# A planner's transfer lengths: by size instead of one length for each transfer

## The chip, the cores and the metric

The kernel runs on one core of a Trainium2 chip. Its engines are TensorE (PE in the profile; PEld is its weight load), VectorE (DVE), ScalarE (ACT), GpSimd (POOL) and SyncE (SP), which here issues the transfers of the main loop. The metric is the device time of one execution in microseconds (us), the median of several runs; lower is better. Times inside an execution come from one profiled run.

## What is computed

Two layers follow each other on an input of 8 images, 192 channels, 64 x 64 pixels, all in float32. The first is a gated scan over four directions, the second an attention over windows of 8 x 8 pixels with an MLP. Cut to what matters:

```python
# layer 0
x = conv1x1(x, W_in)                                  # 192 -> 384 channels
x = depthwise_conv3x3(x, W_dw) + b_dw
proxy = conv1x1(x, W_xd)                              # 384 -> 16
Gl, Gm, Gr = normalize_w(*split(conv1x1(proxy, W_w))) # each / (|Gl|+|Gm|+|Gr|+1e-7)
Ls, Us, Ds = (conv1x1(proxy, w) for w in (W_l, W_u, W_d))
xs = [x, x.T, flip(x), flip(x.T)]                     # four directions
# columns are cut into chunks of 8; the scan runs over the 8 places in a chunk
h = l * x + gl * h_up + gm * h + gr * h_dn
y = sum_d w_m[d] * (out * Us + xs * Ds)
x = conv1x1(grn(layernorm2d(y)), W_out)               # grn: norm over the whole image
# layer 1
s = layernorm(x); q, k, v = s @ qkv_w.T, in windows of 64 tokens, 6 heads
attn = softmax(top16(l2n(q) @ l2n(k).T * temp) + rpb)
x2 = s + (attn @ v) @ proj_w.T
out = x2 + gelu(layernorm(x2) @ fc1_w.T) @ fc2_w.T
```

## The kernel before

Each image passes through three stages, and three images are in work at once.

`front(b)` makes the first two lines. In four reads it loads rows of x into `xt` (L505, L506). For each of three channel tiles ct it projects them on PE, ScalarE copies the result into `xin`, and SP stores that in an HBM buffer `pad` with a border (L539). For the convolution SP loads strips of `pad`, three shifted copies of 132 KB each, into one of two `strip` buffers (L553), and PE multiplies them at L565, 24 matmuls for a strip. ScalarE writes two layouts of the result, `st` and `sn`, and SP stores them in the HBM buffers `xs` and `xsT` (L598, L599). An image has 24 stores of `pad`, 48 strips, and 24 stores each of `xs` and `xsT`. `pad` is there twice, `xs` and `xsT` three times.

`scan(b)` has 8 steps t, each over 12 tiles (direction d, channel tile ct). At the start of a step `proxy` loads all of x0 from `xs` (L631), multiplies it on PE (L638), and carries the small result through HBM (`flat`, L653) to a spread copy `xe` (L661). The nine tiles of directions other than 0 each load an `xd` of 256 KB (L694), in one of four buffers. PE makes the gates at L678; ScalarE, VectorE and GpSimd take their absolute values, normalise them and update the state `hid` between L711 and L807; `dx` and `hu` (L833, L838) are the outputs, and GpSimd sums them into `y3`. `norm` finishes a step, and SP stores it in the HBM buffer `z` (L928). The scan of an image can start only when its whole `xs` is written.

`window_row(b, g)` handles one of the 8 rows of windows: it loads `zg` from `z` into a single buffer (L1032), ScalarE scales it (L1037), PE turns it into tokens (L1052), and then attention and MLP follow up to the stores of `out` (L1513, L1516). It needs the norm over the whole image, so it starts after that image's scan.

None of this is written in the order in which it runs. Every piece is handed to a planner, `Plan`, as a step: engine, cost, function, what it reads and what it writes. `written_down` gives the steps a first rank, so that scan b, windows b - 1 and front b + 1 lie beside each other. `Plan.order` then plays the whole program through 12 times: `run` keeps, for every engine, the time at which it is free, takes the step that can start within 40 ns of that time and has the lowest rank (or else the one that can start first), and notes its start. After each run the rank of a step becomes the latest start that its users allow, and the shortest of the 12 runs wins. The steps are sorted by their planned start, and each engine gets its instructions in that order; from then on the order is fixed, and on the chip only semaphores hold it back.

The cost of a step on any engine but PE is a pair: how long it holds its engine, and how much later its result is there.

```python
hold, more = s.cost
free[e] = t + hold
s.end = free[e] + more
```

SP is such an engine, and a transfer is such a step. Before, `dma(n)` gives n transfers a hold of 350 ns each and 2600 ns more, whatever their size. A user on another engine is ready 70 ns (`HOP`) after that.

Of the kernel before, what the change touches and what calls it, by code (L numbers as in the profile page):

```python
# [288 lines left out]
def tile_ss2d_then_window_attention(ctx: ExitStack, tc: tile.TileContext, a: dict, out: bass.AP):  # L289
# [6 lines left out]
    nc = tc.nc  # L296
# [61 lines left out]
    xt = blank("xt", [P, 3, 8, W])  # L358
# [16 lines left out]
    with tc.tile_pool(name="prep", bufs=2) as prep, tc.tile_pool(name="prep_ps", bufs=2, space=PSUM) as prep_ps:  # L375
# [12 lines left out]
        for n, pair in enumerate(PAIRS):  # L388
            for k, (d, _) in enumerate(pair):
                w = w_g2[64 * k : 64 * k + 64, n * P : (n + 1) * P]  # L390
# [51 lines left out]
        for ci in range(2):  # L442
            w = w_f1[:, ci, :]
# [15 lines left out]
    plan = Plan()  # L459
# [3 lines left out]
    mm = lambda slots, n, share=1.0: (slots * n * 4.0, share)  # L463

    mg = lambda share=1.0: (512 * 5.0 + 240, share)
    dma = lambda n=1: (350.0 * n, 2600.0)
    tiny = (150.0, 90.0)
    log_c = {}
    log_half = blank("log_half", [P, 1], math.log(0.5) / 3)
# [25 lines left out]
    def front(b, xs, xsT):  # L495
        xb = x[b]
        padded = pad[b % 2]

        def read(s):


            def get():
                for k in range(2):
                    rows = slice(8 * (s + k), 8 * (s + k) + 8)
                    nc.sync.dma_start(xt[:, k], xb[0:P, rows, :])  # L505
                    nc.sync.dma_start(xt[64 * k : 64 * k + 64, 2], xb[P:DM, rows, :])  # L506

            plan("SP", dma(4), get, w=["xt", (xs, "room"), (xsT, "room")])

        def project(ct, s):  # L510

            own = padded[ct * P : (ct + 1) * P]
            cols = slice(ct * P, (ct + 1) * P)
            pins = [bank() for _ in range(2)]

            def products():
                outs = [p().rearrange("p (h w) -> p h w", h=8) for p in pins]
                for k in range(2):
                    nc.tensor.matmul(outs[k], lhsT=w_in[:, 0, cols], rhs=xt[:, k], start=True, stop=False)
                for k in range(2):  # L520
                    half = slice(64 * k, 64 * k + 64)
                    nc.tensor.matmul(outs[k], lhsT=w_in[half, 1, cols], rhs=xt[half, 2], start=False, stop=True)

            plan("PE", mm(3, 512), products, r=["xt"], w=pins)
            for k in range(2):
                cur, pin = xin[k], pins[k]
                plan(
                    "ACT",
                    act(512),
                    lambda cur=cur, pin=pin: nc.scalar.copy(  # L530
                        cur[:, :, 1 : W + 1], pin().rearrange("p (h w) -> p h w", h=8)
                    ),
                    r=[pin],
                    w=[("xin", k)],
                )
                plan(
                    "SP",
                    dma(),
                    lambda cur=cur, row=8 * (s + k) + 1: nc.sync.dma_start(own[:, row : row + 8, :], cur),  # L539
                    r=[("xin", k)],  # L540
                    w=[("pad", b % 2, ct, s + k)],
                )

        def convolve(ct, s):

            own = padded[ct * P : (ct + 1) * P]
            pc = bank()
            for k in range(2):
                strip = strips[k]

                def read(row=8 * s + 4 * k, strip=strip):
                    for dy in range(3):
                        nc.sync.dma_start(  # L553
                            strip[dy * RG : (dy + 1) * RG],
                            own[:, row + dy : row + dy + 4, :].rearrange("(q m) h w -> m q (h w)", m=RG),
                        )

                near = [("pad", b % 2, ct, n) for n in range(max(0, s + k - 1), min(NG, s + k + 1))]
                plan("SP", dma(3), read, r=near, w=[("strip", k)])
                rows4 = strip.rearrange("p q (h w) -> p q h w", h=4)  # L560

                def products(k=k, rows4=rows4):
                    for dx in range(3):
                        for q in range(4):
                            nc.tensor.matmul(  # L565
                                pc()[q * RG : (q + 1) * RG, k * 256 : (k + 1) * 256].rearrange("p (h w) -> p h w", h=4),
                                lhsT=w_cv[:, ct, q, dx, :],
                                rhs=rows4[:, q, :, dx : dx + W],
                                start=dx == 0,
                                stop=dx == 2,  # L570
                            )

                plan("PE", mm(3, 256), products, r=[("strip", k)], w=[(pc, k)])
            rows = slice(s * 64, (s + 1) * 64)
            st = Held(fpool, [P, CH, 64], "st")
            plan(
                "ACT",
                (1060.0, 120.0),
                lambda: nc.scalar.activation(
                    st().rearrange("p t (i c) -> p i c t", c=CH),  # L580
                    pc().rearrange("p (i c t) -> p i c t", c=CH, t=CH),
                    AF.Identity,
                    bias=b_dw[:, ct : ct + 1],
                ),
                r=[pc],
                w=[st],
            )
            sn = Held(fpool, [P, 8, W], "sn")
            plan(
                "ACT",  # L590
                act(512),
                lambda: nc.scalar.activation(
                    sn(), pc().rearrange("p (h w) -> p h w", h=8), AF.Identity, bias=b_dw[:, ct : ct + 1]
                ),
                r=[pc],
                w=[sn],
            )
            plan("SP", dma(), lambda: nc.sync.dma_start(xs()[:, ct, :, rows], st()), r=[st], w=[(xs, ct, s)])  # L598
            plan("SP", dma(), lambda: nc.sync.dma_start(xsT()[:, ct, :, rows], sn()), r=[sn], w=[(xsT, ct, s)])  # L599

        for s in range(0, NG + 1, 2):
            if s < NG:
                read(s)
            for ct in range(CT):
                if s < NG:
                    project(ct, s)
                    yield
                for k in range(max(0, s - 1), min(NG, s + 1)):
                    convolve(ct, k)
                    yield  # L610


    def scan(b, xs, xsT, z, made):
# [14 lines left out]
        def proxy(t):  # L628

            x0 = Held(spool, [P, CT, 512], "x0", bufs=1)  # L630
            plan("SP", dma(), lambda: nc.sync.dma_start(x0(), xs()[:, :, t, :]), r=[xs], w=[x0])  # L631
            px = bank()

            def products():
# [19 lines left out]
                r=[xq],  # L654
                w=[flat],
# [6 lines left out]
                r=[flat],  # L662
                w=[xe],
# [7 lines left out]
                r=[xe],  # L671
                w=[xo],
# [9 lines left out]
        def tile_of(t, d, ct, xp, x0, y3, last):  # L682

            ch = d * DIN + ct * P
            if d == 0:
                xd = x0
                flat = lambda: x0()[:, ct, :]
            else:
                xd = Held(spool, [P, 512], "xd", bufs=4)
                src = xs if d == 2 else xsT  # L690
                plan(
                    "SP",
                    dma(),
                    lambda: nc.sync.dma_start(xd(), src()[:, ct, CH - 1 - t if d >= 2 else t, :]),  # L694
                    r=[(src, ct, s) for s in range(NG)],
                    w=[xd],
                )
                flat = lambda: xd()
# [15 lines left out]
            else:  # L714
                g = [bank("g") for _ in range(2)]
# [15 lines left out]
                for r in range(2):  # L731
# [4 lines left out]
                        r=[g[r]],  # L736
                        w=[(ab, r)],
                    )

                def by_state(dst, src, row, n):  # L740
# [13 lines left out]
                    r=[nb, h_key],  # L754
                    w=[(pr, 2)],
                )
                plan("ACT", act(512), lambda: nc.scalar.activation(nb(), nb(), AF.Abs), w=[nb])  # L757
                for r in range(2):
# [4 lines left out]
                        r=[g[r], h_key],  # L763
                        w=[(pr, r)],
# [96 lines left out]
        def norm(t, y3):  # L861
# [14 lines left out]
            def spread(dst, src):  # L876
# [15 lines left out]
                r=[pm],  # L892
                w=[y3],
# [8 lines left out]
            v, r, rr = lambda: pv()[:, 0:P], lambda: sq()[:, 0, 0:P], lambda: sq()[:, 1, 0:P]  # L902
# [7 lines left out]
                r=[sq],  # L910
                w=[pv],
# [5 lines left out]
                r=[pv],  # L917
                w=[sq],
# [6 lines left out]
                r=[pv],  # L925
                w=[y3],
            )
            plan("SP", dma(), lambda: nc.sync.dma_start(z()[:, :, t, :], y3()), r=[y3], w=[(z, t)])  # L928
            for ct in range(CT):
                plan(  # L930
                    "ACT",
# [9 lines left out]
                    r=[y3],  # L941
                    w=[(sq, ct), (gx, ct, t)],
# [11 lines left out]
        for t in range(CH):  # L954
            x0, xe, xo = ready
            y3 = Held(spool, [P, CT, 512], "y3", bufs=2)
# [52 lines left out]
    def window_row(b, g, z, sc, bb):  # L1009
# [19 lines left out]


        zg = Held(lpool, [P, CT, CH, 64], "zg", bufs=1)
        plan("SP", dma(), lambda: nc.sync.dma_start(zg(), z()[:, :, :, g * 64 : (g + 1) * 64]), r=[z], w=[zg])  # L1032

        def scaled_up():
            for ct in range(CT):
# [5 lines left out]
        for t2 in range(2):  # L1041
            pz = bank()
            ss = Held(small, [P, 2], "ss")
            for k in range(2):
# [19 lines left out]
                r=[pz],  # L1064
                w=[(s0, t2)],
            )

            def squares(pz=pz, ss=ss):
# [9 lines left out]
                w=[ss],  # L1078
# [17 lines left out]
        for tt in range(NT):  # L1096
            pq = bank()

            def projected(tt=tt, pq=pq):
# [11 lines left out]
                r=[pq],  # L1111
                w=[(qk, tt)],
# [366 lines left out]
        for ci in range(2):  # L1479
# [35 lines left out]
                    for k in range(2):  # L1515
                        nc.sync.dma_start(o[P:DM, :, 32 * k : 32 * k + 32], ot()[64 * k : 64 * k + 64])  # L1516

            plan("SP", dma(1 + ci), put, r=[ot], w=[("out", b, g, ci)])
            yield
        plan.lane = 1  # L1520

# [110 lines left out]
```

## Time and profile before

| | |
|---|---|
| median of 3 runs | 8295.51 us (8274.17 to 8303.1) |
| the profiled execution, by the clock of the runs | 8293.82 us |
| its span, first to last instruction | 8292.0 us |
| mean granted TensorE clock | 0.827 |
| moved by the 16 DMA engines | 695.70 MB, 84 GB/s in the mean |

The span is what the views of the trace are read against; 1.8 us lie around it. In the views a group has the line, the engine, the tiles as output<-input, and counts or times in us. A wait is written as "engine line <- what ended it: total, times, longest". "PEclk" or "clock" is the share of full speed that TensorE was granted.

The main transfers of the loop, all issued by SP, with their number and size each:

| transfer | line | number | KB each |
|---|---|---|---|
| strip<-pad | L553 | 1152 | 132 |
| xd<-xsT, xd<-xs | L694 | 384 + 192 | 256 |
| pad<-xin | L539 | 192 | 264 |
| xs<-st, xsT<-sn | L598, L599 | 192 + 192 | 256 |
| x0<-xs (x<-xs in the profile) | L631 | 64 | 768 |
| z<-y, zg<-z | L928, L1032 | 64 + 64 | 768 |
| xt<-x | L505, L506 | 64 + 64 | 256, 128 |
| out<-ot | L1513, L1516 | 64 + 128 | 256, 64 |
| flat<-xq, xe<-flat | L653, L661 | 64 + 64 | 64, 256 |

### The profile page before, as it was taken

What the parts mean: (1) busy time and instruction counts of PE and PEld (TensorE: products, weight loads), DVE (VectorE), ACT (ScalarE), POOL (GpSimd) and SP (SyncE); (2) the same over time, 40 slices, a digit from 0 to 9 for tenths busy, and PEclk for the clock granted to TensorE, in tenths of its full rate; (3) what the DMA queues carried; (4) which work ended last, traced back from release to release, by engine and by line L of the source; (5) the groups of instructions that cost most, each with busy time, mean ns of one, the idle gap of its engine ahead of it and who ended that gap; (6) DMA issues with size and microseconds to landing.
All of it is one profiled execution on the core that took longest, in us unless ns stands there. A gap on an engine that the chain in (4) does not pass through costs nothing.

```text
span 8292.0 us, 147108 instructions
## 1 busy us (share of the span) xinstructions
PE 6951.0 (84%) x51224; PEld 3600.7 (43%) x51224; DVE 6381.9 (77%) x15421; ACT 5488.0 (66%) x12537; POOL 5859.7 (71%) x5918
## 2 busy tenths in 40 slices
PE   5677688788988898888988898888888789888887
PEld 2333344444444444444444444444444444444454
DVE  1366777888788987888788887888888888888643
ACT  1355346766677666777577766777677676677787
POOL 0377877788778877788778777778788788877411
PEclk8887579788898788888898889888788887778898
DMA  6776146111542135411532126311111112111110
GB/s 175 193 191 180 42 128 165 50 44 45 139 129 74 52 96 138 107 45 56 157 103 77 46 76 171 91 46 46 57 41 50 43 41 66 41 48 41 30 22 15
DMA packets 1037948, 695.70 MB, mean 84 GB/s; under 512 B 704115, under 2 KB 860214, under 8 KB 1037206
## 3 DMA queue, kind: packets, MB, share of 16 engines
q1 hardware_dynamic: 1035830, 684.99, 30.9%
q8 instruction: 407, 6.67, 0.3%
q14 instruction: 335, 2.74, 0.1%
q10 hardware_dynamic: 1376, 1.30, 0.1%
HBM read 453.43 MB, written 232.67 MB: 83 GB/s over the span
## 4 chain that ended last, share of the span: by engine, by line
PE 23%; ACT 15%; DVE 14%; POOL 9%; DMA 5%; issue 4%; SPq 0%; POOLq 0%; DVEq 0%; ACTq 0%
PE g L678 6%; PE lp L1487 3%; PE lp L1453 2%; ACT at L1286 2%; ACT at L1298 2%; DMA zg<-z 2%; POOL pr L796 2%; PE lp L1052 2%; PE lp L565 2%; DVE pr L742 1%; PE lp L1102 1%; POOL pr L781 1%; ACT ab L735 1%; DMA strip<-pad 1%; POOL ab L766 1%
## 5 line engine op out<-in xcount | busy, mean ns | idle before, releaser
L678 PE MATMUL g<-xe,w_g 32*128 32x512 f32 x3648 | 1281.3, 777 | 284.0 <-DVE dx L833 90.3
L678 PE MATMUL g<-xo,w_g 32*128 32x512 f32 x3648 | 1218.2, 767 | 270.1 <-DVE dx L833 154.0
L796 POOL TENSOR_TENSOR pr<-pr,rr 128x512 f32<-128x512 f32 x672 | 872.5, 1298 | 369.4 <-ACT rr L779 320.5
L781 POOL TENSOR_TENSOR pr<-pr 128x512 f32<-128x512 f32 x672 | 887.2, 1321 | 339.7 <-DVE pr L742 254.8
L766 POOL TENSOR_TENSOR ab<-ab 128x512 f32<-128x512 f32 x672 | 873.4, 1300 | 269.6 <-ACT ab L735 264.7
L735 ACT ACTIVATE ab<-g 128x512 f32<-128x512 f32 x1344 | 778.7, 594 | 295.1 <-PE nb L678 175.5
L847 POOL TENSOR_TENSOR dx<-dx,hu 128x512 f32<-128x512 f32 x576 | 738.8, 1294 | 257.6 <-DVE hu L838 250.8
L565 PE MATMUL lp<-strip,w_cv 128*32 128x256 f32 x9216 | 678.3, 438 | 289.0 <-DMA strip<-pad 265.9
L785 POOL TENSOR_TENSOR pr<-pr 128x512 f32<-128x512 f32 x672 | 884.2, 1316 | 20.6
L678 PEld LDWEIGHTS g<-xe,w_g 32*128 32x128 f32 x3648 | 451.9, 219 | 835.0 <-DVE dx L833 206.5
L678 PEld LDWEIGHTS g<-xo,w_g 32*128 32x128 f32 x3648 | 423.4, 217 | 812.4 <-DVE dx L833 278.4
L777 ACT ACTIVATE rr<-nb,eps 128x512 f32<-128x512 f32 x672 | 460.4, 685 | 436.5 <-DVE nb L774 320.8
L1487 PE MATMUL lp<-hd,w_f 128*64 128x256 f32 (+1 forms) x2304 | 610.1, 505 | 63.4 <-ACT hd L1473 39.7
L792 DVE SCALAR_TENSOR_TENSOR nb<-nb,rr 128x512 f32<-128x512 f32 x672 | 464.7, 692 | 237.6 <-ACT rr L779 236.1
L565 PEld LDWEIGHTS lp<-strip,w_cv 128*32 128x32 f32 x9216 | 313.5, 122 | 659.3 <-issue 388.6
L855 POOL TENSOR_TENSOR y<-y,dx 128x512 f32<-128x512 f32 x384 | 593.9, 1555 | 1.8
L800 DVE SCALAR_TENSOR_TENSOR nb<-nb,pr 128x512 f32<-128x512 f32 x672 | 464.4, 691 | 152.5 <-POOL pr L796 148.1
L774 DVE TENSOR_TENSOR nb<-nb,ab 128x512 f32<-128x512 f32 x672 | 464.7, 691 | 128.9 <-POOL ab L766 98.8
L845 POOL TENSOR_TENSOR y<-hu,dx 128x512 f32<-128x512 f32 x192 | 247.3, 1296 | 418.8 <-DVE hu L838 415.7
L757 ACT ACTIVATE nb<-nb 128x512 f32<-128x512 f32 x672 | 397.8, 592 | 206.5 <-DVE pr L742 107.8
L838 DVE TENSOR_TENSOR hu<-g,hid 128x512 f32<-128x512 f32 x768 | 511.4, 678 | 4.6 <-PE g L678 1.7
L678 PE MATMUL nb<-xe,w_g 32*128 32x512 f32 x672 | 506.4, 844 | 8.8 <-DVE hid L807 8.6
(202 smaller groups left out, 17104.4 us busy)
## 6 DMA issues: line engine op xcount, KB each, us to landing
strip<-pad SPq DMA_DIRECT2D x1152, 132.0 KB
xd<-xsT SPq DMA_DIRECT2D x384, 256.0 KB
pad<-xin SPq DMA_DIRECT2D x192, 264.0 KB
xs<-st SPq DMA_DIRECT2D x192, 256.0 KB
xsT<-sn SPq DMA_DIRECT2D x192, 256.0 KB
xd<-xs SPq DMA_DIRECT2D x192, 256.0 KB
x<-xs SPq DMA_DIRECT2D x64, 768.0 KB
z<-y SPq DMA_DIRECT2D x64, 768.0 KB
```

The source lines that it names most:

```text
L565: nc.tensor.matmul(pc()[q * RG : (q + 1) * RG, k * 256 : (k + 1) * 256].rearrange("p (h w) -> p h w", h=4), lhsT=w_cv[:, ct, q, dx, :], rh ...
L678: nc.tensor.matmul(dst, lhsT=w[rows, col : col + P], rhs=xp[rows, :], start=True, stop=True)
L735: lambda r=r: nc.scalar.activation(ab()[:, r, :], g[r](), AF.Abs),
L766: plan("POOL", gp(512), lambda: nc.gpsimd.tensor_add(ab()[:, 0, :], ab()[:, 0, :], ab()[:, 1, :]), w=[ab])
L774: plan("DVE", vec(512), lambda: nc.vector.tensor_add(nb(), nb(), ab()[:, 0, :]), r=[ab], w=[nb])
L781: plan("POOL", gp(512), lambda: nc.gpsimd.tensor_add(one(), one(), pr()[:, 1, :]), r=[(pr, 1)], w=[(pr, 0)])
L785: lambda: nc.gpsimd.tensor_add(one(), one(), pr()[:, 2, :]),
L796: plan("POOL", gp(512), lambda: nc.gpsimd.tensor_mul(one(), one(), rr()), r=[rr], w=[(pr, 0)])
L838: lambda: nc.vector.tensor_mul(like(hu(), d), like(pu(), d), state(d, ct)),
L847: plan("POOL", gp(512), lambda: nc.gpsimd.tensor_add(dx(), dx(), hu()), r=[hu], w=[dx])
L855: nc.gpsimd.tensor_add(y, y, dx().rearrange("p (c i) -> p i c", c=CH))
L1487: nc.tensor.matmul(dst[:, at : at + rhs.shape[-1]], lhsT=lhsT, rhs=rhs, **flags)
```

## The change

`dma` gets a second argument, the size in KB. The hold of a transfer step is now the larger of 350 ns for each transfer and 5.4 ns for each KB; the 2600 ns that follow stay. Ten steps are given a size; the steps of `flat` and `xe` are left without one and keep their 350 ns. Some sizes are larger than the bytes that are moved: 360 for 256 KB of `xs` and `xsT`, 900 for 768 KB of `zg`. Instructions, buffers and dependencies are as before.

```diff
-    dma = lambda n=1: (350.0 * n, 2600.0)
+    dma = lambda n=1, kb=0: (max(350.0 * n, 5.4 * kb), 2600.0)
...
-            plan("SP", dma(4), get, w=["xt", (xs, "room"), (xsT, "room")])
+            plan("SP", dma(4, 786), get, w=["xt", (xs, "room"), (xsT, "room")])
...
-                    dma(),
+                    dma(1, 264),
                     lambda cur=cur, row=8 * (s + k) + 1: nc.sync.dma_start(own[:, row : row + 8, :], cur),
...
-                plan("SP", dma(3), read, r=near, w=[("strip", k)])
+                plan("SP", dma(3, 396), read, r=near, w=[("strip", k)])
...
-            plan("SP", dma(), lambda: nc.sync.dma_start(xs()[:, ct, :, rows], st()), r=[st], w=[(xs, ct, s)])
-            plan("SP", dma(), lambda: nc.sync.dma_start(xsT()[:, ct, :, rows], sn()), r=[sn], w=[(xsT, ct, s)])
+            plan("SP", dma(1, 360), lambda: nc.sync.dma_start(xs()[:, ct, :, rows], st()), r=[st], w=[(xs, ct, s)])
+            plan("SP", dma(1, 360), lambda: nc.sync.dma_start(xsT()[:, ct, :, rows], sn()), r=[sn], w=[(xsT, ct, s)])
...
-            plan("SP", dma(), lambda: nc.sync.dma_start(x0(), xs()[:, :, t, :]), r=[xs], w=[x0])
+            plan("SP", dma(1, 768), lambda: nc.sync.dma_start(x0(), xs()[:, :, t, :]), r=[xs], w=[x0])
...
-                    dma(),
+                    dma(1, 256),
                     lambda: nc.sync.dma_start(xd(), src()[:, ct, CH - 1 - t if d >= 2 else t, :]),
...
-            plan("SP", dma(), lambda: nc.sync.dma_start(z()[:, :, t, :], y3()), r=[y3], w=[(z, t)])
+            plan("SP", dma(1, 768), lambda: nc.sync.dma_start(z()[:, :, t, :], y3()), r=[y3], w=[(z, t)])
...
-        plan("SP", dma(), lambda: nc.sync.dma_start(zg(), z()[:, :, :, g * 64 : (g + 1) * 64]), r=[z], w=[zg])
+        plan("SP", dma(1, 900), lambda: nc.sync.dma_start(zg(), z()[:, :, :, g * 64 : (g + 1) * 64]), r=[z], w=[zg])
...
-            plan("SP", dma(1 + ci), put, r=[ot], w=[("out", b, g, ci)])
+            plan("SP", dma(1 + ci, 256 >> ci), put, r=[ot], w=[("out", b, g, ci)])
```

## The prediction, made before the changed kernel ran

> **What bounds the kernel now.** I read the page first, its busy shares and its forty slices, then busy time by stage, then the waits of TensorE and ScalarE, then the chain of waits, and last the timeline of SP, which issues every transfer of the loop.
>
> ```profile
> PE 6951.0 (84%) x51224; PEld 3600.7 (43%) x51224; DVE 6381.9 (77%) x15421; ACT 5488.0 (66%) x12537; POOL 5859.7 (71%) x5918
> ...
> DMA  6776146111542135411532126311111112111110
> GB/s 175 193 191 180 42 128 165 50 44 45 139 129 74 52 96 138 107 45 56 157 103 77 46 76 171 91 46 46 57 41 50 43 41 66 41 48 41 30 22 15
> ```
>
> No engine is full, and the transfers are dense only in the first four slices and then in humps, one for each image's front (projection and convolution). By stage (PE, weight loads, DVE, ACT, POOL, then granted clock, share of the DMA engines, GB/s):
>
> ```profile
> 20.00:265.00 245.00, 143.77 (x1288) 65.54 (x1288) 8.65 (x29) 51.54 (x73) 0.00 (x0) 0.79 0.68 175
> 265.00:800.00 535.00, 411.71 (x3524) 178.82 (x3524) 324.43 (x510) 259.90 (x432) 355.46 (x280) 0.84 0.74 196
> 800.00:1170.00 370.00, 255.59 (x986) 124.67 (x988) 274.80 (x430) 139.25 (x249) 304.66 (x242) 0.56 0.20 60
> ...
> 4951.00:5915.00 964.00, 850.05 (x6503) 446.13 (x6500) 795.99 (x1927) 686.21 (x1579) 739.12 (x744) 0.85 0.32 85
> 5915.00:6868.00 953.00, 807.06 (x5403) 433.13 (x5402) 818.44 (x2044) 669.40 (x1606) 743.96 (x764) 0.82 0.17 47
> 6868.00:7780.00 912.00, 776.87 (x5362) 411.51 (x5362) 792.20 (x1982) 649.90 (x1532) 719.86 (x739) 0.81 0.16 44
> 7780.00:8292.00 512.00, 415.90 (x3642) 258.79 (x3640) 216.27 (x1048) 393.01 (x1054) 83.46 (x248) 0.89 0.10 23
> ```
>
> The first is front 0 alone, the second fronts 1 and 2 beside scan 0, the third scan 0 alone. Then one row for each image whose scan runs beside the windows of the image before; the last is the windows of image 7 alone. The reader should compare the row of 964 (with a front) with those of 953 and 912 (without): the five images with a front take 949 us in the mean, those without 932, though the DMA share is double. So in the 6610 us from 1170 to 7780 transfers set little; three engines at 75 to 90% that wait for one another set the pace. Only the first 800 us lean on transfers. The waits (total, times, longest) say the same:
>
> ```profile
> PE lp L565 <- DMA strip<-pad: 265.9, 90, 9.1
> PE g L678 <- DVE dx L833: 244.3, 136, 7.6
> PE lp L638 <- DMA x<-xs: 60.2, 27, 4.3
> ...
> ACT zg L1037 <- DMA zg<-z: 98.9, 37, 7.4
> ```
>
> Of the 265.9, 93.2 lie before 265, 90.1 between 265 and 800, 82.6 after 1170. What single transfers take, from the chain (start, length):
>
> ```profile
> 2516.46 4.03 DMA strip<-pad
> ...
> 2699.43 5.03 DMA x<-xs
> ...
> 2841.95 5.77 DMA zg<-z
> ```
>
> Last, the pace of scan 0, by its stores z, one for each step t:
>
> ```profile
> 506.20 1.34 SPq L928 DMA_DIRECT2D z<-y  x1
> 627.17 0.59 SPq L928 DMA_DIRECT2D z<-y  x1
> 747.80 0.57 SPq L928 DMA_DIRECT2D z<-y  x1
> ...
> 856.04 0.58 SPq L928 DMA_DIRECT2D z<-y  x1
> 958.57 0.58 SPq L928 DMA_DIRECT2D z<-y  x1
> 1060.32 0.58 SPq L928 DMA_DIRECT2D z<-y  x1
> 1166.51 0.59 SPq L928 DMA_DIRECT2D z<-y  x1
> ```
>
> A step takes 121 us beside a front and (1166.51 - 856.04)/3 = 103.5 us alone. The second number is the issue's own time on SP, about 0.6 us: near the old 350 ns, and far from the length of a transfer.
>
> **The Trainium skill.** "DMA: Bandwidth & Descriptors", section "Anatomy of one DMA — SWDGE (gpsimd) path", says that DMA engines do not wait on semaphores: the wait is on the issuing sequencer. Here SP waits at L694 (xd) for DVE 1681.3 us in all, and nothing behind such a wait is issued: SP's order counts, and it is the planner's. "PSUM — Partial Sum Buffer", section "Engine vs sequencer instructions", says that the queues of ScalarE, VectorE and GpSimdE are strict FIFO and that matmuls start in program order. The ninety strip waits agree: a convolution that the plan puts too early holds all of PE. "Why small descriptors are slow" on the DMA page puts the overhead of a 256-byte piece at 27%. The trace's packets took 18.5 ns for 256 bytes and 106.7 ns for 2048, so 1.39 times as long per byte; the change writes 360 KB for such a 256 KB transfer, 1.41 times.
>
> **The change, part by part.** No instruction is added, removed or resized. A planner's SP step has a hold (SP taken) and 2600 ns more until its data is there; the hold goes from 350 ns for each DMA to 5.4 ns for each KB. What can change is order alone: which of 12 planned orders wins, and where in each engine's queue a step stands. So its direct cost is nothing and every gain is a wait avoided.
>
> Holds of one image, from counts by the loops: reads of x, 4 of 4.24 us; pad 24 of 1.43; strips 48 of 2.14; xs and xsT 48 of 1.94. The front sums to 17.0 + 34.2 + 102.6 + 93.3 = 247.1 us, where it was 5.6 + 8.4 + 50.4 + 16.8 = 81.2. One step t: x0 4.15, nine xd at 1.38, z 4.15, flat and xe as before 0.70, together 21.4; a window row: zg 4.86, out 2.08, together 6.9. An image is then 247.1 + 8 x 28.4 = 474 us of SP, where it was 129.
>
> *Front 0.* On the chip it lasts 245 us, the new plan's 247 and not 81. Yet it fills those 245 us with its own transfers at 175 GB/s, and nothing else can run before scan 0. Bounds: 10 us lost to 10 gained; I take 0.
>
> *265 to 800.* The plan now knows that two fronts take about 500 us, so matmuls on strips move back behind scan 0's. The upper bound is scan 0 at its pace alone: 17.3 us over some 4.3 steps, 75. The bytes remain and the front still competes for PE and ACT, so I take a quarter, 20; the lower bound is a loss, the rival's below.
>
> *x0.* The transfer takes about 5.0 us, the old plan says 2.95 and the new 6.75, so nearly all of PE's 39.2 us of waits between 1170 and 7780 should go. What is late next is DVE's dx, which PE already waits for 244.3 us; half comes back. Take 20, bounds 0 and 39.
>
> *Strips after 1170.* 82.6 us in 40 waits. The planned length goes from 3.65 to 4.74 us against 4.03 seen unloaded. As images with a front cost only 17 us more than those without, most is given back: take 10, bounds 0 and 40.
>
> *zg.* 98.9/37 = 2.7 us a wait, just what the old plan lacks (5.77 - 2.95). With 7.46 it is covered. ACT is 66% busy, and only what stands behind on ACT while DVE or PE starve counts: a fifth, 20, bounds 0 and 85.
>
> *What the new plan gets wrong.* Pessimism about zg (7.46 for 5.77) and x0 holds single buffers longer on paper, and any reordering makes waits of its own. Take 10 lost.
>
> The sum is 20 + 20 + 10 + 20 - 10 = 60 us. Against the profiled execution (8293.8 us by the clock of the runs, its span 8292.0) that is 8234, and with the median of the three runs 1.7 above it 8235. Buffers and engine work stay the same. xe and flat keep their 2.95, though a chain step shows xe at 8.21 us, so their 29 us of PE waits stay.
>
> **Rivals.** *Full cover, 8150.* Scan 0 gets the whole 75, x0 its 39, the strips 20 and zg 10: 144. For it: each wait's shortfall matches the old plan's error. Against it: the small difference between images with and without a front.
>
> *Nothing, 8295.* DVE and POOL, at 80 to 90% in the quiet slices, keep the pace, so waits on transfers only change name. For it: the 932 us of images without a front. The order would differ and the time would not.
>
> *SP full on paper, 8366, slower.* The planner lets one transfer hold SP for its whole length, where the chip frees SP after 0.3 to 0.6 us and overlaps transfers. Its 5.4 ns for a KB is 190 GB/s, which the stage 265 to 800 exceeds (196) with the engines at 0.74. That stage asks on paper for 2 x 247.1 + 4.5 x 21.4 = 590 us of SP in a stretch of 535, and front 3's hump (1100 to 1400) for 247 + 2.5 x 28.4 = 318 in 300: 55 and 18 too much. If scan steps stand behind such paper queues, the work that needs them is ordered late on every engine: +73, 8293.8 + 73 = 8366. It decides where scan's x0 and xd come after strips and not by rank ahead of them. Against it: after the first of the 12 runs rank is the latest start that its users allow, which puts the scan first; in a usual hump of 380 us the demand is only 247 + 3.1 x 28.4 = 335. Chance reordering ends in this region as well.
>
> **How the numbers follow.** Forecast (8235, own range 8185 to 8270) 0.40; full cover 0.14; nothing 0.16; SP full 0.30. About 0.3%, 25 us, is what a measurement of this kernel can tell from no change. Faster takes the first two and a little of the third, 0.55; same 0.15; slower 0.30. The range runs from just under full cover to just over the paper queue, 8140 to 8375, with 0.2 outside: bounds that exceed the cover, and reorderings worse than the rival.
>
> **What would show it.** Right: waits PE on x<-xs under 20 us in all, ACT on zg<-z under 40, scan 0's z stores 115 to 118 us apart before 800, busy times within 1%. Full cover: stores at 104 to 108. SP full: stores above 121 or front 2 ending well after 800, and DVE and POOL idle in the humps. Nothing: these waits fall and the image's 945 us stays. I am wrong in my main step if the transfer waits fall and the waits between PE, DVE, ACT and POOL grow by more.

## The result, and the profile after

| | before | after |
|---|---|---|
| median | 8292.89 us | 8098.4 us |
| ratio, 95% interval | | 0.9769 [0.9754, 0.9784] |
| span of the profiled execution | 8292.0 us | 8104.4 us |
| end of scan 0 (its last z store) | 1167 | 1087 |
| from there to the last z store of scan 7 | 6614 | 6470 |
| from there to the end | 512 | 547 |

The changed kernel is 194 us faster, where 60 were forecast. Of the table's last three rows, the stage up to the end of scan 0 gave 80, the one from there to the last z store (below: the steady stage) 144, and the last stage took back 35. From the first two parts of the changed kernel's page:

```profile
PE 6948.0 (86%) x51224; PEld 3591.2 (44%) x51224; DVE 6375.0 (79%) x15421; ACT 5491.1 (68%) x12537; POOL 5856.9 (72%) x5918
...
DMA  7765444311543144412343124331211111111010
GB/s 185 183 168 164 112 133 127 92 41 49 154 123 79 44 124 111 118 46 79 105 129 81 42 85 131 87 92 50 57 47 42 51 56 48 48 46 44 23 25 13
```

The instructions are the same in number and busy time to 0.1%: only waiting went. The first hump of transfers is lower and longer, the valley after it is filled (the fifth slice: 42 GB/s before, 112 now). By stage, cut at the changed kernel's own z stores after the second row:

```profile
20.00:265.00 245.00, 152.62 (x1314) 67.32 (x1315) 8.65 (x29) 52.16 (x74) 0.00 (x0) 0.78 0.72 184
265.00:800.00 535.00, 446.86 (x3179) 188.52 (x3177) 382.09 (x599) 271.87 (x458) 417.93 (x330) 0.80 0.63 169
...
5732.00:6656.00 924.00, 791.38 (x5312) 424.66 (x5310) 798.89 (x1923) 646.03 (x1520) 731.21 (x745) 0.82 0.17 48
6656.00:7557.00 901.00, 789.24 (x5408) 423.85 (x5408) 806.62 (x2021) 667.82 (x1603) 734.56 (x754) 0.84 0.17 46
7557.00:8104.00 547.00, 440.74 (x3892) 275.76 (x3890) 226.34 (x1140) 407.74 (x1090) 85.33 (x261) 0.88 0.09 21
```

From 265 to 800 GpSimd, which the scan needs, works 418 us instead of 355, while the transfers run at 169 GB/s instead of 196. The images without a front, too, fell, from 953 and 912 us to 924 and 901, but that is no more than another order of the old lengths can bring: the first kernel of the experiments has 925 and 903 there, the second 958 and 961. The waits of PE and of ACT:

```profile
PE g L678 <- DVE dx L833: 195.1, 114, 7.3
PE lp L565 <- DMA strip<-pad: 128.8, 50, 8.0
...
PE g L678 <- DMA xe<-flat: 14.9, 8, 4.0
...
ACT zg L1037 <- DMA zg<-z: 3.0, 3, 1.5
```

PE's waits on x<-xs are down to 2.3 us. Of the 128.8 on strips, 85.7 lie in front 0, 24.1 between 265 and 800, and 12.3 in the steady stage. Summed over all rows of that view, PE waited for transfers 376.8 us before and 170.7 after; for ACT, DVE and POOL together 936.8 before and 953.8 after. That is the account of the 188 us of span: 206 less of transfer waits, 17 more of the rest. The chain of waits shows it by engine, first before, then after:

```profile
PE 23%; ACT 15%; DVE 14%; POOL 9%; DMA 5%; issue 4%; SPq 0%; POOLq 0%; DVEq 0%; ACTq 0%
PE 19%; ACT 14%; DVE 12%; POOL 11%; issue 3%; DMA 0%; POOLq 0%; DVEq 0%; ACTq 0%; SPq 0%
```

The shares don't sum to the whole span, because the chain could be followed back only to 2514 us before and to 3286 us after. From 3286 us on in both, DMA has 331 us of it before and 21 after. And the steps of scan 0, by their z stores in SP's timeline:

```profile
419.62 0.58 SPq L928 DMA_DIRECT2D z<-y  x1
477.15 0.57 SPq L928 DMA_DIRECT2D z<-y  x1
588.83 0.58 SPq L928 DMA_DIRECT2D z<-y  x1
681.32 0.58 SPq L928 DMA_DIRECT2D z<-y  x1
779.54 0.58 SPq L928 DMA_DIRECT2D z<-y  x1
899.83 0.58 SPq L928 DMA_DIRECT2D z<-y  x1
987.54 0.57 SPq L928 DMA_DIRECT2D z<-y  x1
1087.08 0.57 SPq L928 DMA_DIRECT2D z<-y  x1
```

From 477 on a step takes (1087.08 - 477.15)/6 = 101.7 us although fronts still run beside it; that is about the pace that scan 0 had alone before (103.5). Single steps are uneven, 58 to 120 us, and the first store comes later than before (420 us instead of 386). Front 2 made room: its reads of x stand at 562, 613, 701 and 775 us, before at 480, 562, 623 and 681.

### The profile page after: what moved, and what is told of

Same layout as the page of the kernel before. It is cut to its first block, busy times and chain, and to the rows that moved or that the text cites. A ratio compares the mean times of both kernels' runs of the same rounds, so it can differ in the third digit from the quotient of the medians.

```text
span 8104.4 us, 147053 instructions
## 1 busy us (share of the span) xinstructions
PE 6948.0 (86%) x51224; PEld 3591.2 (44%) x51224; DVE 6375.0 (79%) x15421; ACT 5491.1 (68%) x12537; POOL 5856.9 (72%) x5918
## 4 chain that ended last, share of the span: by engine, by line
PE 19%; ACT 14%; DVE 12%; POOL 11%; issue 3%; DMA 0%; POOLq 0%; DVEq 0%; ACTq 0%; SPq 0%
PE g L678 5%; PE lp L1487 3%; PE lp L1453 2%; POOL pr L796 2%; ACT at L1286 2%; ACT at L1298 2%; POOL ab L766 2%; POOL pr L781 2%; PE lp L1102 2%; POOL dx L847 1%; POOL pr L785 1%; ACT hd L1473 1%; DVE pr L742 1%; PE lp L1457 1%; DVE nb L800 1%
## 5 line engine op out<-in xcount | busy, mean ns | idle before, releaser
L678 PE MATMUL g<-xe,w_g 32*128 32x512 f32 x3648 | 1278.2, 771 | 250.3 <-DVE dx L833 89.9
L678 PE MATMUL g<-xo,w_g 32*128 32x512 f32 x3648 | 1216.6, 744 | 293.5 <-DVE dx L833 105.1
L735 ACT ACTIVATE ab<-g 128x512 f32<-128x512 f32 x1344 | 779.4, 594 | 276.0 <-PE nb L678 109.3
L678 PEld LDWEIGHTS g<-xe,w_g 32*128 32x128 f32 x3648 | 456.0, 216 | 791.6 <-DVE dx L833 202.9
L565 PE MATMUL lp<-strip,w_cv 128*32 128x256 f32 x9216 | 675.4, 436 | 147.5 <-DMA strip<-pad 128.8
L678 PEld LDWEIGHTS g<-xo,w_g 32*128 32x128 f32 x3648 | 421.0, 210 | 845.3 <-DVE dx L833 223.4
L777 ACT ACTIVATE rr<-nb,eps 128x512 f32<-128x512 f32 x672 | 460.8, 686 | 467.6 <-DVE nb L774 337.3
L757 ACT ACTIVATE nb<-nb 128x512 f32<-128x512 f32 x672 | 397.9, 592 | 224.2 <-DVE pr L742 121.8
L678 PE MATMUL nb<-xe,w_g 32*128 32x512 f32 x672 | 513.8, 855 | 5.9 <-DVE hid L807 5.9
```

Of the source, the lines that this page charges most:

```text
L565: nc.tensor.matmul(pc()[q * RG : (q + 1) * RG, k * 256 : (k + 1) * 256].rearrange("p (h w) -> p h w", h=4), lhsT=w_cv[:, ct, q, dx, :], rh ...
L678: nc.tensor.matmul(dst, lhsT=w[rows, col : col + P], rhs=xp[rows, :], start=True, stop=True)
L735: lambda r=r: nc.scalar.activation(ab()[:, r, :], g[r](), AF.Abs),
```

## The experiments

Theory A: each planned length, and the planned load on SP, mends the waits that it concerns, and a wait that goes is gained nearly whole. The rivals: B, any new order of this program beats the one before, which was an unlucky draw; C, only the load on SP counts; D, the prediction's, that most of a wait that goes comes back under another name. The kernel before was timed again beside each group, with medians of 8286 to 8290 us, and gains are counted from these; the 95% intervals of the gains reach 8 to 16 us to either side. The columns on stages and waits come from one profiled execution of each kernel, which can lie some 25 us off its median. Of "PE on strip", PE's waits on strip<-pad, some 90 us lie in front 0 in every kernel. A kernel that is planned with all but the same lengths and so comes out in another order is called a new draw.

### Is it chance?

Two kernels give the planner another number that says nothing new, and two do the same to the changed kernel.

```diff
# first and second, against before
-    dma = lambda n=1: (350.0 * n, 2600.0)
+    dma = lambda n=1: (345.0 * n, 2600.0)
+    dma = lambda n=1: (350.0 * n, 2610.0)
# third and fourth, against the changed kernel
-    dma = lambda n=1, kb=0: (max(350.0 * n, 5.4 * kb), 2600.0)
+    dma = lambda n=1, kb=0: (max(345.0 * n, 5.45 * kb), 2600.0)
+    dma = lambda n=1, kb=0: (max(350.0 * n, 5.4 * kb), 2610.0)
```

> The kernel before with every transfer held 345 ns instead of 350, which says nothing true or false about lengths but lets the planner fall into another order. Theory A (each part of the change mends its own waits): the kernel before is a usual plan of its kind, so 8240 to 8340, scan 0 ending at 1150 to 1180, PE's waits on strips near 266 and ACT's on zg near 99 us. Theory B (the plan before was an unlucky draw, and any new draw is faster): below 8220.

> The kernel before with 2610 ns of lateness instead of 2600. As the run before: theory A 8240 to 8340 with the waits of before, theory B below 8220. The two together with the kernel before show how far a re-draw alone moves the time.

> The changed kernel with 5.45 ns for each KB instead of 5.4 and 345 ns instead of 350. Theory A: 8050 to 8150, scan 0 ending at 1080 to 1100 and few waits on zg and x. Theory B: anywhere from 8050 to 8300.

> The changed kernel with 2610 ns of lateness instead of 2600. Theory A: 8050 to 8150 as before; the last stage, which took 547 us in the changed kernel and 503 to 524 in all others, falls back to about 520, if its length was an accident of that one order. Theory B: anywhere from 8050 to 8300.

| | median us | ratio to before | scan 0 ends | steady | last stage | ACT on zg |
|---|---|---|---|---|---|---|
| before, 345 ns | 8297.06 | 1.0013 [1.0003, 1.0022] | 1175 | 6597 | 517 | 94 |
| before, 2610 ns | 8304.91 | 1.0021 [1.0011, 1.0032] | 1161 | 6651 | 501 | 100 |
| changed, 5.45 ns | 8068.59 | 0.974 [0.9725, 0.9754] | 1081 | 6481 | 513 | 2 |
| changed, 2610 ns | 8028.72 | 0.9692 [0.9674, 0.971] | 1073 | 6445 | 501 | 3 |

B falls: the two new draws of the kernel before stay within 19 us of it, with nearly its waits (PE's on all transfers 337 and 342 us instead of 377, without being faster for it). The changed kernel and its two draws go from 8029 to 8098, the changed kernel being the slowest of the three and 8029 lying below what A expected; its last stage of 547 us isn't found in the other two. So an order's accident weighs up to 70 us here, and a difference of that size between two single kernels is not proof by its size alone.

### Which transfers

The front's five sizes alone, and the five of scan and windows alone (the others as before):

```diff
# front alone, against the changed kernel: x0, xd, z, zg, out
-dma(1, 768)   dma(1, 256)   dma(1, 768)   dma(1, 900)   dma(1 + ci, 256 >> ci)
+dma()         dma()         dma()         dma()         dma(1 + ci)
# scan and windows alone: x, pad, strip, xs, xsT
-dma(4, 786)   dma(1, 264)   dma(3, 396)   dma(1, 360)   dma(1, 360)
+dma(4)        dma()         dma(3)        dma()         dma()
```

> Sizes for the front's transfers alone (x, pad, strip, xs, xsT); x0, xd, z, zg and out keep 350 ns each. Theory A (each part of the change mends its own waits): scan 0 gets the stage before 1100 us, its last z store at about 1090 instead of 1167, PE's strip waits fall to about 130 us in all as with the whole change, but PE's waits on x<-xs stay near 60 us and ACT's on zg<-z near 99; time about 8180 to 8210. Theory B (chance: any new planning of this program lands somewhere within about 1% of before): no part of this pattern, the stage of scan 0 not near 1090. Theory C (only the load on SP in the plan counts): 8110 to 8150, as most of that load is the front's.

> Sizes for x0, xd, z, zg and out alone; the front's transfers keep 350 ns each. Theory A: scan 0 still ends at about 1165 and PE's strip waits stay near 266 us, but PE's waits on x<-xs and ACT's on zg<-z nearly go (under 10 us each); time about 8170 to 8210, so that the two halves add up to the whole. Theory B: no such pattern. Theory C: 8240 to 8290.

Then scan and windows once more in three pieces: zg alone, x0 alone, and xd, z and out.

> A size for zg alone (one of ten). Theory A (each length mends its own wait): ACT's waits on zg<-z fall from 95 us to under 10, all other transfer waits stay; of the 155 us that the sizes of the scan and window transfers together brought, zg brings 50 to 100, so 8190 to 8245. Theory D (as the prediction had it: a wait of ScalarE that goes is mostly given back): 8265 to 8285.

> A size for x0 alone. Theory A: PE's waits on x<-xs fall from some 55 us to under 5, the rest stays, and 30 to 60 us are gained: 8230 to 8260. Theory D (half given back): 8265 to 8280.

> Sizes for xd, z and out alone, on which hardly anybody waits in the kernel before. Theory A: no wait to mend, so 8270 to 8310. If the planned load on SP in the scan were worth something by itself: 8200 to 8250.

| sizes given | median us | less than before | scan 0 ends | steady | PE on strip | PE on x | ACT on zg |
|---|---|---|---|---|---|---|---|
| none (before) | 8290 | | 1167 | 6614 | 266 | 60 | 99 |
| front | 8190.94 | 99 | 1097 | 6552 | 150 | 40 | 92 |
| scan, windows | 8134.64 | 155 | 1138 | 6459 | 225 | 1 | 1 |
| zg | 8223.73 | 65 | 1168 | 6551 | 224 | 53 | 7 |
| x0 | 8214.86 | 74 | 1138 | 6570 | 239 | 2 | 117 |
| xd, z, out | 8265.53 | 23 | 1136 | 6621 | 241 | 40 | 78 |

In the waits of the kernel with zg's size alone that wait is gone, and the others stand or fall by less:

```profile
PE lp L565 <- DMA strip<-pad: 223.6, 83, 8.6
PE lp L638 <- DMA x<-xs: 52.8, 22, 5.3
PE g L678 <- DMA xe<-flat: 22.9, 7, 7.1
...
ACT zg L1037 <- DMA zg<-z: 6.6, 6, 2.2
```

In those of the kernel with the front's sizes alone it is the other way round:

```profile
PE lp L565 <- DMA strip<-pad: 150.1, 54, 7.8
PE lp L638 <- DMA x<-xs: 39.8, 20, 5.3
...
ACT zg L1037 <- DMA zg<-z: 92.2, 38, 6.6
```

Each size takes its own wait away, as A says. C isn't decided here: its ranges took most of the load to be the front's, but by the prediction's own sums the front takes 247 of an image's 474 us. It falls below, with a kernel that has before's load on SP and is 169 us faster. D doesn't fit: beside 92 us less of ScalarE's waits on zg the kernel is 65 us faster, beside 58 less of PE's on x0 74, beside 116 less on strips 99. Of A's ranges of time those for the front and for zg were met; scan and windows came out 35 us below theirs, x0 15, and xd, z and out 4.

How much of the 65 and the 74 is the edit's own is less sure, as they are about the size of an accident. Strip waits fell by 42 and 27 us in these two kernels though no strip was given a length, as they did by 16 and 24 in the new draws of before, and with zg's size PE's waits on ScalarE did not fall (429.8 to 434.0). Nor is the earlier end of scan 0 (1138) shown to be x0's doing: the kernel with xd, z and out sized has it too (1136). What does tell the waits apart is the chain of waits, taken from 2514 us on, as far as it goes in before: zg<-z has 149 us of it in before, 9 with zg's size and 152 with x0's; x<-xs has 73 in before, 64 with zg's size and none with x0's (strip<-pad falls from 106 to 39 and 37, but to 41 also in the second new draw of before). So both waits were on the path that ended last, and each left it with its own length.

The 23 us of the last row, where there was little to mend, is about what a new draw moves. The two halves sum to 254 us, more than the changed kernel's 194 and close to its best draw's 257.

### Length or load

A hold does two things: the result comes later, and SP is taken for other transfers. The first kernel keeps the change's planned end and frees SP. The second keeps SP taken and takes the added hold off the 2600 ns, as far as these reach: strips keep before's 3.65 us and xd its 2.95, but x0 and z are planned at 4.15 and zg at 4.86. The third has no sizes but one longer length for all.

```diff
-    dma = lambda n=1, kb=0: (max(350.0 * n, 5.4 * kb), 2600.0)
+    dma = lambda n=1, kb=0: (350.0 * n, 2600.0 + max(0.0, 5.4 * kb - 350.0 * n))
+    dma = lambda n=1, kb=0: (max(350.0 * n, 5.4 * kb), max(0.0, 2600.0 - max(0.0, 5.4 * kb - 350.0 * n)))
# against before
-    dma = lambda n=1: (350.0 * n, 2600.0)
+    dma = lambda n=1: (350.0 * n, 4650.0)
```

> The same ends of transfers as in the change, but SP held for only 350 ns for each: the size goes into the lateness of the result. If the planned length of a transfer is what helps, about 8100 and all transfer waits as in the changed kernel. If the planned load on SP is what helps, scan 0 ends late again (about 1165) because the plan still takes the front's transfers for free in bandwidth, the waits on zg<-z and x<-xs go all the same, and the time is about 8190 to 8220.

> The holds of the change, but the lateness cut by the same amount, so that a transfer that needn't queue ends when it did before (2.95 us for most). If the planned load on SP is what helps, scan 0 ends at about 1090 and the time is near 8130 to 8170, with waits on zg<-z and x<-xs partly back (zg planned at 4.9 against 5.8 on the chip). If the planned length is what helps, about 8250 to 8290.

> No sizes: every transfer keeps 350 ns of hold and gets 4650 ns of lateness instead of 2600, 5.0 us in all, about what x0 takes on the chip. If lengths have to go by size, this is worse than the lateness by size (8122): small transfers are planned too late and it lands at 8180 to 8290. If any longer length does, 8100 to 8150, with waits on x<-xs, xe<-flat and strips small and some left on zg<-z; scan 0 ends near 1130 as with lateness by size, since the planned load on SP is that of before.

| | median us | less than before | scan 0 ends | steady | PE on strip | ACT on zg |
|---|---|---|---|---|---|---|
| length alone, by size | 8121.61 | 169 | 1130 | 6478 | 208 | 2 |
| load alone, by size | 8061.0 | 229 | 1079 | 6461 | 119 | 20 |
| one longer length | 8094.62 | 194 | 1113 | 6460 | 196 | 29 |

Busy time from 265 to 800 of the kernel with length alone:

```profile
265.00:800.00 535.00, 437.98 (x3540) 188.01 (x3541) 348.38 (x549) 267.28 (x448) 386.68 (x305) 0.84 0.73 195
```

The transfers keep before's share and rate here (0.74, 196 GB/s); this is the stage that needs the load, though C, by which only load counts, falls. With the front's load scan 0 ends at 1073 to 1097 in every kernel at 5.4 ns or near it, without it at 1113 and later. The steady stage is shortened by either. The second kernel doesn't part load from length for x0 and zg, which it plans longer than before, but for strips it does: with their old length of 3.65 us, PE waits 119 us for them instead of 266, where the length alone left 208. My expectations for the load alone, "8250 to 8290" or "8130 to 8170", were both too low a gain. And the size-blind kernel reaches 8095, 5 us below what was expected if any longer length does: for the steady stage one longer length does as well as lengths by size.

### How long, how loaded, and the one wait left

```diff
-    dma = lambda n=1, kb=0: (max(350.0 * n, 5.4 * kb), 2600.0)
+    dma = lambda n=1, kb=0: (max(350.0 * n, 5.4 * kb), 3600.0)   # first
+    dma = lambda n=1, kb=0: (max(350.0 * n, 3.7 * kb), 2600.0)   # third
+    dma = lambda n=1, kb=0: (max(350.0 * n, 8.0 * kb), 2600.0)   # fourth
# second, the steps of flat and xe
-dma()        dma()
+dma(1, 64)   dma(1, 512)
```

> The changed kernel with 3600 ns of lateness instead of 2600, so every transfer is planned 1 us longer than in the change (zg 8.5, x0 7.7, strips 5.7 us). If pessimism has a price (the prediction took 10 us), 8100 to 8150; if slack is nearly free, 8010 to 8070, within the spread of the changed kernel and its two re-draws (8029 to 8098), with the strip waits outside front 0 near 0.

> The changed kernel with lengths for flat and xe as well, which the change left at 2.95 us (xe planned at 5.4 us, as the chain of before shows it). Each length mends its own wait: PE's waits on xe<-flat fall from 15 to 21 us to under 5; with that some 10 to 20 us off the middle of the changed kernel and its re-draws (8065), so 8020 to 8080. If a re-draw by itself weighs more: anywhere from 8020 to 8110.

> The changed kernel with 3.7 ns for each KB instead of 5.4, about what the chip's DMA engines take when they are busy (685 MB in 30.9% of the span). If the planned load on SP is what gives scan 0 its stage, that stage lies between: its end at 1090 to 1125; zg is planned at 5.9 us and x0 at 5.4, just what they take, so their waits stay small; 8060 to 8120.

> 8 ns for each KB. The plan's SP is then at 0.7 ms an image of some 0.92. If the load that the prediction's slower rival feared has a price (work that stands behind queues which exist on paper alone), it shows here: above 8130, with fronts that end much later and scan steps late in the humps. If rank keeps the scan ahead, 8030 to 8100 and scan 0's end at 1065 to 1090.

| | median us | ratio to before | scan 0 ends | steady | PE on strip | PE on xe |
|---|---|---|---|---|---|---|
| 1 us longer | 8094.55 | 0.9766 [0.9751, 0.978] | 1097 | 6470 | 123 | 10 |
| flat and xe sized | 8009.12 | 0.9662 [0.9647, 0.9676] | 1077 | 6401 | 111 | 2 |
| 3.7 ns for a KB | 8067.7 | 0.9737 [0.9718, 0.9755] | 1102 | 6414 | 194 | 19 |
| 8 ns for a KB | 8088.99 | 0.9756 [0.9739, 0.9772] | 1109 | 6457 | 108 | 20 |

The changed kernel with flat and xe sized as well is the fastest of all, 278 us under before and 89 under the changed kernel; against that one's best draw it is 20, so only the wait that went (15 to 2 us) is shown to be its doing. At 3.7 ns some of the strip waits come back (194 instead of 129) and scan 0 ends later, as expected, yet the time is in the midst of the changed kernel's draws: not every wait has its price in every order. At 8 ns the fronts stretch (front 2 begins at 719 us instead of 562), and from 265 to 800 there is this:

```profile
265.00:800.00 535.00, 439.23 (x2579) 183.55 (x2578) 375.61 (x592) 244.56 (x422) 412.74 (x326) 0.73 0.48 130
```

Transfers at 0.48, yet scan 0 isn't faster than with 5.4 ns. Its steps, from its first z store to its last, take 95 us in both (111 before); only its first store is later (444 us), and it ends at 1109 where 1065 to 1090 was expected. Both the 1 us and the 8 ns kernels are within the spread of the changed kernel's draws. Whether planning too long costs a little (29 and 24 us over the mean of those draws, 8065) or nothing, these runs don't settle.

What a wait is worth in the mean, all 18 kernels together say better than any two of them. A straight line through their median times, against PE's waits on transfers plus ScalarE's on zg, has a slope of 0.80 us for each us of wait (0.81 for PE's and 0.77 for ScalarE's where each has its own), and the kernels lie 32 us about it (root mean square). So about four fifths of such a wait is gained, over many orders; for a single one the accident of the order can hide it.

## Why the prediction was wrong in size

*Direct cost nothing, gains only from avoided waits*: right; busy times moved by 0.1%, PE's transfer waits fell by 206 us.

*Front 0, 0 us*: right; its strip waits went only from 93.2 to 85.7.

*265 to 800, "so I take a quarter, 20"*: this term failed. The stage brought 80 by the end of scan 0, above the bound of 75. The bytes and engine work that I had reasoned with do remain, but part of them moved into the valley after 800: from there to the end of scan 0 the DMA engines were at 0.20 and are now at 0.41. They can move, because nobody needs front 2's data before scan 2 starts at about 2000 us.

*x0, "half comes back. Take 20"*: failed; with its size alone the kernel is 74 us faster, 44 of it in the steady stage and 29 before scan 0's end, the 29 not shown to be its own. PE's waits on dx did not grow in their place: in the changed kernel they went from 244.3 to 195.1.

*Strips, 10*: failed; the front's sizes brought 62 in the steady stage, where the strip waits went from 82.6 to 24.

*zg, "a fifth, 20"*: failed; with its size alone the kernel is 65 us faster, beside 92 us of waits that went, and zg<-z left the chain of waits. What I counted was how busy ACT is. What I left out is its order: ScalarE's queue is strict FIFO, as the Trainium skill says ("PSUM — Partial Sum Buffer", section "Engine vs sequencer instructions"). In before's trace, of the six ScalarE instructions that come next behind each of the 37 late zg, 54 of 222 are the scan's absolute values, logarithms and exponentials (L735, L757, L777, L779). That this is the whole reason isn't shown.

*Pessimism, -10*: neither shown nor excluded; lengths that are longer still cost 24 to 29 us or nothing.

Behind all of these lies one misreading. I took the 949 us of images with a front and the 932 of those without as proof that transfers set little, and set these 17 us, which are for one image, against 82.6 us of strip waits, which are for five: over five images the difference is 85 us, as much as the waits. Nor can it prove anything either way: in the two new draws of before it is 40 and -13 us. And both kinds of image wait for x0 and zg, which are no part of the front (6 and 13 us an image with a front, 4 and 10 without), so the comparison couldn't show these waits at all. Last, engines at 75 to 90% left room: PE's waits for the other engines did not grow in place of those that went (936.8 to 953.8).

Of the signs that I named, the waits on x and zg and the busy times came as for "right"; the z stores before 800, 101 us apart in the mean from 477 on, lie even below full cover's 104 to 108.

Of the rivals, "full cover, 8150" named the mechanism and was too small. "SP full on paper" shows at 8 ns in the fronts, which stretch, but not in its cost: scan 0 ended 57 us sooner than before and the time stayed 198 us under before. "Nothing" is excluded by the result, and chance by the new draws.

## What to carry to other kernels

Where a planner orders in-order queues by hand-given lengths, compare each planned length with what the trace shows and make none too short: of the waits on transfers that went, here 2 or 3 us for each, about four fifths was gained, and those of ScalarE, 66% busy, counted like those of TensorE. Lengths that are too long cost little here, and one generous length did as well as lengths by size, save in the stage where the transfers of the fronts crowd the scan; there the plan needs their load. Before putting a per cent down to such an edit, draw the same plan again with a number that means nothing: here that alone moved the time by 19 to 70 us.

## What the runs showed of the hardware that was not expected

In the stage 265 to 800 the kernel with 8 ns for a KB has 2579 matmuls in 439 us of busy PE at a granted clock of 0.73, the changed kernel 3179 in 447 us at 0.80. The gate matmuls (L678) are as many in both, 725 and 731; the strip matmuls, all of one shape, are not (the changed kernel first, then 8 ns; count, then busy us and mean ns):

```profile
L565 PE MATMUL lp<-strip,w_cv 128*32 128x256 f32 x1824 | 146.1, 470 | 28.0 <-DMA strip<-pad 24.1 <-DVE pr L744 2.0 <-ACT rr L777 1.9
L565 PE MATMUL lp<-strip,w_cv 128*32 128x256 f32 x1272 | 115.4, 520 | 12.1 <-DMA strip<-pad 12.1
```

A matmul of the same shape was recorded as longer at the lower clock, 520 ns instead of 470 (the profile models the ends of matmuls). So PE was about as busy while it did three tenths less of the convolution, and its busy share alone would not have shown that.
